# Layer 0's adjacency normalised with a graph in each partition, and group 0's sums read back in 128 rows

## The chip, the cores and the metric

The kernel runs on one core of a Trainium2 chip. The metric is the device time of one execution in microseconds (us), as the median of several runs. Engines are named as in the profile: PE is TensorE, DVE is VectorE, ACT is ScalarE, POOL is GpSimd, SP is the engine whose queue issues most of the transfers.

## The reference, cut to what matters

Four graph layers follow one another over 128 graphs of 64 nodes with 256 features, each with a residual and a layer norm. The change lies in layer 0. It works on the first 25 nodes of each graph, in five groups of nodes that overlap; each group has its own two-step graph convolution, and the groups' outputs are added with weights:

```
GROUPS = [list(range(25)), [0..8], [0, 9..14], [6, 7, 8, 12, 13, 14], [3, 4, 5, 9, 10, 11]]
def graph_conv(x, adj, W, b):
    A = adj + eye(n);  deg = sum(A, -1)
    dinv = where(deg == 0, 0, deg ** -0.5)
    return relu((dinv[:, :, None] * A * dinv[:, None, :]) @ (x @ W) + b)
for g, idx in enumerate(GROUPS):
    h = graph_conv(x[:, idx], adj[:, idx][:, :, idx], W1[g], b1[g])
    fused[:, idx] += softmax(fusion_w)[g] * graph_conv(h, adj_g, W2[g], b2[g])
x = layernorm(x + fused)          # nodes 25 to 63: only the norm of x
```

Layers 1 and 2 (a normalised convolution and a polynomial in the adjacency) and layer 3 (five steps of a gated recurrent cell over the graph) follow. Everything is float32.

## The kernel before, in words

**Units.** Layer 0 is cut into 16 units of up to four tiles. A tile holds as many graphs of one group as fit in the partitions, one row per node: 14 graphs of 9 nodes (group 1, units 0 to 2), 16 of 7 (group 2, units 3 and 4), 21 of 6 (groups 3 and 4, units 5 to 8), and 5 of 25 (group 0, units 9 to 15). For a unit i the steps are:

- `load0` brings the nodes' features xg (L447) and, for group 1, the rows of the adjacency a (L443).
- The block-diagonal, normalised and transposed adjacency AT is made in one of two ways. `prep` (L456) does it for units 0 to 2: identity, degree, power, the spread to blocks (L484), a transpose on TensorE (L492), and the second factor at the eviction (L497). For the others, `norm_group` (L517) normalises a whole group at once for all 128 graphs, in AL and AU, where each strip of 32 partitions holds nodes and 32 graphs lie along the row; VectorE's 32x32 block transpose (L533) turns it, SP stores it to DRAM as nt (L541), `load_turned` (L547) reads it back in the unit's row order, and `spread_out` (L561) multiplies it into blocks (L571).
- `aggregate` (L590) multiplies xg and AT; `hidden` (L606) or, from unit 3 on, `hidden7` (L629) multiplies by W1. `hidden7` takes seven products in place of eight, which need factors of W1 (`factors0`, L616, on POOL) and sums t of the aggregate (L634 to L636, on POOL), and copies c that ACT makes and DVE adds to (L665, the tile hg).
- `supports` (L685) multiplies by W2, `add` (L711) by AT again; its result z is added into F, the sums of groups 1 to 4, and for group 0 the sums F are added to z (L725).
- The sums of group 0 must come back from features-in-partitions to nodes-in-partitions. `finish` does it by TensorE's transpose (L778) for units 9, 14 and 15; for units 10 to 13, `turn_sum` (L739) turns z in 32x32 blocks on DVE (L744), stores it as zd (L748) and reads it back as zr (L750); `finish_turned` (L756) adds it (L759) and normalises.

`others` (L824) normalises nodes 25 to 63 in ten pieces, loaded by `load_others` (L799), stored as xb (L829).

**Order.** TensorE's instructions run in the order of the program throughout; from unit 2 on ACT, DVE and POOL do too, and that order is written out by hand in ORDER0 (L68), a row for each unit: P and F are `add` and its sum, A is `aggregate` of the next unit, digits are the products of `hidden7`, b, g, d and c its evictions, S is half of `supports`, L the loads for three units on, X `spread_out` for two units on, q a piece of the norms, e a piece of `mid`, the layers 1 and 2 of the first two chunks. SP's order, and all orders before unit 2, come from the scheduler, by its own costs and by priorities. [...]

**Shared places.** AL and AU have the tag RZ with two buffers; `ih` and `wl`, into which POOL loads the weights of layer 3 three at a time from unit 5 on (`moves`, L1040), take the same two buffers and wait until AL and AU are free. `a` has three buffers, xg five, W1 and W2 two each.

Of the kernel before, what the change touches and what calls it, by code (L numbers as in the profile page):

```python
# [28 lines left out]
NE = 15  # L29
# [36 lines left out]
WAITS = 6  # L66

ORDER0 = """  # L68
P A S q L 1 X 2 F 6 5 q 7 g S q 4 d 3 b c S S
A S 1 q q L q X q 2 5 q q 6 q S 7 P q S 4 q g q 3 q q S F b c d  # L70
q q A L P 1 S q S 6 2 q X 5 q q q 7 S S g F q b 4 q q 3 d c
A S P q L 1 X q S 6 F q q 2 5 q 7 q g S S 4 b q 3 q d c q q q
A P L 1 X S 6 2 q q 5 q S 7 F S q q 4 q g q q q d q q q b 3 c q S
X A q L P q S 1 q q q q q S q 6 F 2 q S q q 5 q q b q 7 q q S g 4 d 3 c
A q L q S X 1 S q 6 P 2 5 q 7 g S b 4 q q q d F q 3 q q S c q q
L X A P S 1 S 2 q 6 S 5 7 S q q q g 4 F 3 d q b c q
X P A L S 1 2 F q 6 5 q q q e 7 b g q q S q e 4 3 S q q q c S e q d e
X A L P 1 F 2 e q S 6 S q q b e e 5 q 7 S e g q q q 4 3 c S q e d e
L X P e A 1 F q S S 2 e e 6 5 q 7 q S q b q e 4 g q q q 3 e q S q d c q e e
L A e X P 1 2 F S 6 q q q q 5 S e 7 e S q g q 4 b q 3 q d q q S c q e q  # L80
X A S 1 e e L P 2 e e F 6 b 5 q q q q S 7 e g 4 S e q d q 3 q q q q e q c q e e S e
A L X e S 1 P 6 e q e q q q 2 5 F b e 7 S q q S 4 q e q e q g q q q 3 q e q S d c e
# [28 lines left out]
def gnn_stack(  # L111
# [305 lines left out]
    with ExitStack() as c0:  # L417
# [9 lines left out]
        def load0(i, after=None):  # L427
# [3 lines left out]
            qa = {0: [nc.sync, nc.scalar, nc.gpsimd, nc.sync], 1: [nc.sync, nc.scalar]}.get(i, [nc.sync])  # L431
            qx = nc.gpsimd if i < 3 else nc.sync
            a = work.tile([TR, 4, NJ], F32, name="a", bufs=3) if u.g == 1 else None
            xg = work.tile([TR, 4, D], F32, name="xg", bufs=5)
            w = u.n if u.g < 2 else NE
# [6 lines left out]
            for rows, t, b, f in runs if u.g == 1 else ():  # L442
                qa[t % len(qa)].dma_start(a[rows, t, :w], adj[b, f, 0:w])  # L443
# [12 lines left out]
        def prep(i):  # L456

            u = UNITS[i]
            a, xg = loads.pop(i)
            ae = work.tile([TR, 4, NJ], F32, name="ae", bufs=2)  # L460
            A0 = work.tile([TR, 4, TR], F32, name="A0", bufs=1)
            AT = work.tile([TR, 4, TR], F32, name="AT", bufs=4)
            p = psum0("pT").rearrange("p (t n) -> p t n", t=4)
            scale, last = [], evictions[-1] if evictions else None
            for ts, nb, r, k in u.same:
                w, c = ts.stop - ts.start, 0

                step = w if i else 2
                parts = [slice(t, min(t + step, ts.stop)) for t in range(ts.start, ts.stop, step)]
                for f, m in [(0, u.n)] if u.g < 2 else RUNS[u.g]:  # L470
                    with tc.issue_after(last.ins) if last else nullcontext():
                        nc.vector.tensor_add(
                            ae[:r, ts, c : c + m], a[:r, ts, f : f + m], eye0[:r, k, None, c : c + m].to_broadcast([r, w, m])
                        )
                    c += m
                av = ae[:r, ts, : u.n]
                deg = small.tile([TR, w], F32, name="deg")
                nc.vector.tensor_reduce(deg[:r], av, AX.X, ALU.add)
                dinv = inv_sqrt(deg[:r], w, r, "d0")
                nc.vector.tensor_mul(av, av, dinv[:, :, None].to_broadcast([r, w, u.n]))  # L480
                for ps in parts:
                    o, c, n = 0, 0, ps.stop - ps.start
                    for _, m in RUNS[u.g]:
                        nc.vector.tensor_mul(  # L484
                            A0[:r, ps, o : o + nb * m].rearrange("p t (b n) -> p t b n", n=m),
                            ae[:r, ps, None, c : c + m].to_broadcast([r, n, nb, m]),
                            block0[:r, None, k, o : o + nb * m].rearrange("p t (b n) -> p t b n", n=m)
                            .to_broadcast([r, n, nb, m]),
                        )
                        o, c = o + nb * m, c + m  # L490
                    for t in range(ps.start, ps.stop):
                        nc.tensor.transpose(p[:r, t, :r], A0[:r, t, :r], ident[:r, :r])  # L492
                    d = dinv[:, ps.start - ts.start : ps.stop - ts.start, None]
                    scale.append((AT[:r, ps, :r], p[:r, ps, :r], d.to_broadcast([r, n, r])))
            for v in scale:
                with tc.high_priority():
                    evictions.append(nc.vector.tensor_mul(*v))  # L497
            A[i] = AT, xg

        def identity(m):  # L500
            nc.vector.tensor_add(AL[:, :, :m], AL[:, :, :m], eye1[:, None, :m].to_broadcast([128, 32, m]))

        def degrees(g):

            deg = roots[:, 0, max(g - 1, 0)]
            if g == 2:
                nc.vector.tensor_reduce(deg, AL[:, :, 9:15], AX.X, ALU.add)
                nc.vector.tensor_add(deg, deg, AL[:, :, 0])
            elif g:
                seg = AU[:, 16:18, :].rearrange("p b n -> p (b n)").rearrange("p (b s) -> p b s", s=2)  # L510
                for s, (f, m) in enumerate(RUNS[g]):
                    nc.vector.tensor_reduce(seg[:, :, s], AL[:, :, f : f + m], AX.X, ALU.add)
                nc.vector.tensor_add(deg, seg[:, :, 0], seg[:, :, 1])
            else:
                nc.vector.tensor_reduce(deg, AL[:, :, 0:NJ], AX.X, ALU.add)

        def norm_group(g):  # L517

            n, o = len(GROUPS[g]), 0
            S = AS[len(nts) % 2]  # L520
            nts[g] = []
            degrees(g)
            deg, s, r = (roots[:, v, max(g - 1, 0)] for v in range(3))
            nc.vector.scalar_tensor_tensor(s, deg, 0.0, deg, op0=ALU.is_equal, op1=ALU.add)
            powers.append(nc.gpsimd.tensor_tensor(r, s, mhalf[:, :1].to_broadcast([128, 32]), ALU.pow))
            for _ in range(WAITS):
                yield
            nc.vector.scalar_tensor_tensor(s, deg, 0.0, r, op0=ALU.not_equal, op1=ALU.mult)
            d = s[:, :, None]
            for f, m in RUNS[g]:  # L530
                nc.vector.tensor_mul(S[:, :, f : f + m], AL[:, :, f : f + m], d.to_broadcast([128, 32, m]))
            yield
            nc.vector.transpose(AU.rearrange("p b n -> p (b n)"), S.rearrange("p b n -> p (b n)"))  # L533
            yield
            for f, m in RUNS[g]:
                nc.vector.tensor_mul(S[:, :, o : o + m], AU[:, :, f : f + m], d.to_broadcast([128, 32, m]))
                o += m
            for f, m in RUNS[g]:
                nt = dram.tile([B, m, n], F32, name=f"nt{g}{f}")
                for v in range(4):  # L540
                    nc.sync.dma_start(  # L541
                        nt[32 * v : 32 * v + 32].rearrange("b j i -> j b i"), S[32 * v + f : 32 * v + f + m, :, :n]
                    )
                nts[g].append(nt)
            yield

        def load_turned(i):  # L547
            u = UNITS[i]
            a = work.tile([TR, 4, NJ], F32, name="a", bufs=3)
            for ts, nb, _, _ in u.same:  # L550
                row, b0 = 0, u.tiles[ts.start][0]
                w = ts.stop - ts.start
                for nt, (_, m) in zip(nts[u.g], RUNS[u.g]):
                    nc.sync.dma_start(
# [184 lines left out]
        def turn_sum(i):  # L739
# [7 lines left out]
            for v in range(4):  # L747
                nc.sync.dma_start(zv[v], zt[32 * v : 32 * v + 32])  # L748
            zr = work.tile([TR, 4, D], F32, name="zr", bufs=1)
            nc.sync.dma_start(zr[: u0], zd[: 4 * u0].rearrange("(t r) d -> r t d", r=u0))  # L750
# [101 lines left out]
        def load_first(g):  # L852
            W1[g] = w0.tile([128, 2, HID], F32, name="W1", bufs=2)
            nc.sync.dma_start(W1[g], w1[g].rearrange("(k p) e -> p k e", p=128))
# [6 lines left out]
        nts, turned = {}, {}  # L861
        r1 = keep.tile([128, 2, 1024], F32, tag="RZ", name="AL", bufs=2).rearrange("p s (b n) -> p s b n", b=32)
        r2 = keep.tile([128, 2, 1024], F32, tag="RZ", name="AU", bufs=2).rearrange("p s (b n) -> p s b n", b=32)
        AL, AU, AS = r1[:, 0], r1[:, 1], [r2[:, 0], r2[:, 1]]
        eye1 = w0.tile([128, 32], F32, name="eye1")
        roots = w0.tile([128, 3, 4, 32], F32, name="roots")
        nc.vector.memset(AL, 0.0)

        def load_graphs(n, m):

            for v in range(4):
                nc.sync.dma_start(
                    AL[32 * v : 32 * v + n, :, :m], adj[32 * v : 32 * v + 32, :n, :m].rearrange("b i j -> i b j")
                )
# [13 lines left out]
        def stage(f, i, first=0):  # L888
            if first <= i < NU:
                f(i)  # L890
# [12 lines left out]
        for i in range(-2, NU + 1):  # L903
            if i == 2:
                written.enter_context(tc.manual_schedule(engines=free))
            if i == 1:
                factors0(2)
            if i == 0:
                first = norm_group(2)
# [712 lines left out]
```

## Time and profile before

| | us |
|---|---|
| median of three runs (2147.01 to 2149.83) | 2149.17 |
| the profiled execution's own time | 2147.78 |
| its span | 2146.0 |
| PE busy | 2099.1 |
| DVE busy | 1705.3 |
| ACT busy | 1001.0 |
| POOL busy | 653.6 |
| PE busy in the first 345 us, which hold layer 0 and the hand-over to layer 3 | 316.5 |

The mean granted TensorE clock was 0.991. The span is what the records cover; the profiled execution's own time has 1.8 us more around it. In a timeline, a line gives the start, the length, the engine (or its queue: SPq, POOLq, ACTq), the line of the program, the operation, output and inputs with their number, and in brackets the idle time before it and what ended it. In an answer by windows, a line gives the stretch, its length, the busy time of PE, PE's weight loads, DVE, ACT and POOL, then the granted TensorE clock, the share of the 16 DMA engines that were busy, and GB/s.

### The profile page before, as it was taken

The page shows a single profiled execution, that of the slowest core. Times are in us where ns is not written, and L with a number is a line of the kernel's source. Part 1 is how long each engine was busy: PE and PEld are TensorE (multiplying, and loading weights), DVE is VectorE, ACT ScalarE, POOL GpSimd, SP SyncE. Part 2 cuts the span into 40 slices and gives each one's busy share as a digit, 9 for nine tenths or more (in the row PEclk, how much of TensorE's full clock was granted, in tenths as well). Part 3 has the DMA queues.
Part 4 walks back from the last instruction along what each step waited for, and adds up shares of the span by engine and source line. Part 5 has one row for each costly group of instructions (what it writes and reads, how often), then busy time and mean ns, then how long its engine had stood idle before and what let it go on. Part 6 is the DMA issues. An engine that isn't in the chain of part 4 may idle for free.

```text
span 2146.0 us, 31812 instructions
## 1 busy us (share of the span) xinstructions
PE 2099.1 (98%) x10814; PEld 1843.2 (86%) x10814; DVE 1705.3 (79%) x3825; ACT 1001.0 (47%) x2097; POOL 653.6 (30%) x693
## 2 busy tenths in 40 slices
PE   9989889999999999999999999999999999999997
PEld 6879778898888888888888888888889888888886
DVE  4755666787897889788988898879888887888776
ACT  3545334444544445444544454445444454445453
POOL 7543212222232223232322322323322232223222
PEclk9999999999999999999999999999999999999999
DMA  6553220212522243223331332134312431224121
GB/s 174 151 143 83 68 71 21 70 40 55 108 65 51 60 79 86 50 52 74 87 74 40 74 86 68 45 73 86 79 45 55 90 84 40 59 59 97 44 59 40
DMA packets 551488, 154.73 MB, mean 72 GB/s; under 512 B 516160, under 2 KB 546350, under 8 KB 551326
## 3 DMA queue, kind: packets, MB, share of 16 engines
q1 hardware_dynamic: 546294, 147.46, 29.0%
q0 software_dynamic: 2320, 4.82, 0.9%
q8 instruction: 86, 1.41, 0.3%
q10 hardware_dynamic: 2712, 0.42, 0.1%
q14 instruction: 76, 0.62, 0.1%
HBM read 85.12 MB, written 67.49 MB: 71 GB/s over the span
## 4 chain that ended last, share of the span: by engine, by line
PE 79%; DVE 12%; DMA 4%; SPq 2%; issue 1%; POOL 1%; ACT 0%; DVEq 0%; POOLq 0%; ACTq 0%
PE parz L1168 22%; PE pdrz L1168 11%; PE pan L1168 11%; PE pa L272 8%; PE pdn L1168 5%; PE pbrz L1168 5%; PE pd L351 5%; PE ps L685 3%; PE pbn L1168 3%; PE ph L651 2%; DMA zr<-zd 1%; DVE NI L1326 1%; PE pp L332 1%; PE pf L881 1%; DVE NI L1327 1%
## 5 line engine op out<-in xcount | busy, mean ns | idle before, releaser
L1148 POOL TENSOR_TENSOR Ta<-agg 128x512 f32<-128x512 f32 x80 | 104.3, 1303 | 663.8 <-ACT agg L274 663.8
L1269 ACT ACTIVATE RZ<-RZ,brz 128x256 f32<-128x256 f32 x474 | 214.7, 501 | 169.0 <-DVE RZ L1192 168.3
L1168 PE MATMUL parz<-Th,WHH 128*128 128x256 f32 x960 | 288.6, 382 | 3.7 <-ACT c L1188 3.7
L1168 PE MATMUL parz<-Ta,V 128*128 128x256 f32 x960 | 285.5, 379 | 0.0
L1188 ACT COPY c<-parz 128x512 f32<-128x512 f32 x240 | 138.9, 579 | 269.2 <-PE parz L1168 268.3
L1284 ACT ACTIVATE NI<-NI,bih 128x256 f32<-128x256 f32 x316 | 149.2, 504 | 159.6 <-DVE NI L1327 159.5
L1188 ACT COPY c<-pan 128x512 f32<-128x512 f32 x237 | 138.2, 583 | 182.0 <-PE pan L1168 182.0
L1168 PEld LDWEIGHTS parz<-Th,WHH 128*128 128x128 f32 x960 | 179.6, 190 | 35.8 <-ACT c L1188 12.7
L1168 PEld LDWEIGHTS parz<-Ta,V 128*128 128x128 f32 x960 | 182.4, 190 | 24.8
L1148 POOL TENSOR_TENSOR Th<-hn 128x512 f32<-128x512 f32 x64 | 81.5, 1273 | 314.6 <-DVE hn L1291 310.3
L1289 DVE TENSOR_TENSOR RZ<-hn,NI 128x256 f32<-128x256 f32 x252 | 134.0, 532 | 34.5 <-ACT NI L1284 34.1
L1290 DVE TENSOR_TENSOR RZ<-RZ 128x256 f32<-128x256 f32 x316 | 150.9, 478 | 10.7
L1192 DVE TENSOR_TENSOR NI<-pdn,c 128x512 f32<-128x512 f32 x158 | 108.2, 685 | 56.7 <-ACT c L1188 54.6
L188 POOL TENSOR_TENSOR rs<-ve,mhalf 128x4 f32<-128x4 f32 (+2 forms) x65 | 69.5, 1070 | 256.4 <-DVE ve L181 187.1
L1327 DVE TENSOR_TENSOR NI<-NI 128x256 f32<-128x256 f32 x237 | 138.6, 585 | 8.2
L1168 PE MATMUL pan<-Ta,V 128*128 128x256 f32 x474 | 144.1, 385 | 0.1
L1168 PE MATMUL pan<-Th,WHH 128*128 128x256 f32 x474 | 141.0, 379 | 0.0
L1192 DVE TENSOR_TENSOR RZ<-pdrz,c 128x512 f32<-128x512 f32 x160 | 109.6, 685 | 37.1 <-PE pdrz L1168 25.3
L1326 DVE SCALAR_TENSOR_TENSOR NI<-NI,bhh,RZ 128x256 f32<-128x256 f32 x237 | 128.3, 541 | 6.3 <-ACT RZ L1269 1.4
L274 ACT COPY agg<-pa 128x512 f32<-128x512 f32 x160 | 93.3, 585 | 76.9 <-PE pa L272 76.3
L272 PEld LDWEIGHTS pa<-A,h 128*128 128x128 f32 x1024 | 124.5, 192 | 5.0 <-DMA h<-hb 1.6
L272 PE MATMUL pa<-A,h 128*128 128x128 f32 x1024 | 124.9, 275 | 1.5 <-DMA h<-hb 1.5
(267 smaller groups left out, 4874.8 us busy)
## 6 DMA issues: line engine op xcount, KB each, us to landing
hb<-flip SPq DMA_DIRECT2D x184, 256.0 KB
h<-hb SPq DMA_DIRECT2D x624, 64.0 KB
out_dram<-xt SPq DMA_DIRECT2D x30, 256.0 KB
hT<-hb SPq DMA_DIRECT2D x112, 64.0 KB
W<-in_w_dram SPq DMA_DIRECT2D x10, 512.0 KB
xt<-xb SPq DMA_DIRECT2D x32, 156.0 KB
xo<-in_x_dram SPq DMA_DIRECT2D x9, 512.0 KB
xb<-xo SPq DMA_DIRECT2D x9, 512.0 KB
```

The costliest lines, as they stand in the source:

```text
L272: nc.tensor.matmul(p[:, q * 128 : (q + 1) * 128], src(q, k), m[:, q, :], start=True, stop=True)
L351: nc.tensor.matmul(p[:, h, :], ag[:, k, q * 128 : (q + 1) * 128], W[:, k, :], start=k == 0, stop=k == 1)
L1148: nc.gpsimd.tensor_sub(t[:, 0:2, :], a[:, :, H:], a[:, 0, :].rearrange("p (s n) -> p s n", s=2))
L1168: nc.tensor.matmul(bank[:, g, :], w[:, q, i - 1, :], rhs, start=i in (1, 2, 5) and g == 0 and m == 0, stop=m == len(side) - 1, skip_group_ ...
L1188: nc.scalar.copy(c, self.a)
L1192: nc.vector.tensor_add(v, self.b if i == 2 else self.d, self.copies.pop({7: 7, 2: 1, 3: 6}[i]))
L1269: nc.scalar.activation(v, self.g.a[:, q, :] if i == 4 else v, AF.Sigmoid, bias=brz[:, 2 * q + j : 2 * q + j + 1])
L1284: nc.scalar.activation(n, n, AF.Tanh, bias=bih[:, 4 + j : 5 + j])
L1289: nc.vector.tensor_sub(d, self.hT[:, j, f], n)
L1290: nc.vector.tensor_mul(d, d, z)
L1326: nc.vector.scalar_tensor_tensor(n[:, j, f], h, bhh[:, 4 + j : 5 + j], r[:, j, f], op0=ALU.add, op1=ALU.mult)
L1327: nc.vector.tensor_add(n[:, j, f], i, n[:, j, f])
```

## The change

Only unit 0 keeps its adjacency from `prep`. For all groups, `norm_group` now works with one graph in each partition: AL holds the 25 used rows of each graph as they lie in DRAM, loaded in two pieces (rows 0 to 8, rows 9 to 24). The identity is added along the diagonal by one step with a stride of 65. Groups 2 to 4 are first copied together (L503 of the changed kernel); a degree sum, the guarded power of n columns, one product into S, and one product into T, whose operand S is read with its two inner axes exchanged, so that no block transpose is needed. T is stored as nt with one DMA for each run of nodes. Groups 2, 3, 4 and 0 are done together at unit 0; group 0 was done from unit 4 on. Units 1 and 2 take the way of `load_turned` and `spread_out`.

`turn_sum` stores zd and reads zr with priority; zr is four reads of 128 rows (rows t*125 to t*125+127, the last three of each unused) where it was one of 125 rows by four. ORDER0 has new rows. The loads of the other pieces, of W1 (with priority from group 2 on) and W2 have new places, the weight moves no longer wait for a power in the scheduler's order, and `load_adj(0)` comes after a read-back.

```diff
-WAITS = 6
 ORDER0 = """
-P A S q L 1 X 2 F 6 5 q 7 g S q 4 d 3 b c S S
-A S 1 q q L q X q 2 5 q q 6 q S 7 P q S 4 q g q 3 q q S F b c d
...
-L A e X P 1 2 F S 6 q q q q 5 S e 7 e S q g q 4 b q 3 q d q q S c q e q
...
+X q A P 1 q S L 2 6 5 b 7 S q g S F 3 4 c S d q
+X A S 1 2 q q 5 6 S L q q P 7 q S g q 4 F 3 q c S b q d
...
+X A e e P 1 2 L F 6 S q q q q e q 5 S 7 q S g b q 3 q 4 q d c q S q e q
...
@@ load0
-            qa = {0: [nc.sync, nc.scalar, nc.gpsimd, nc.sync], 1: [nc.sync, nc.scalar]}.get(i, [nc.sync])
+            qa = [nc.sync, nc.scalar, nc.gpsimd, nc.sync]
-            a = work.tile([TR, 4, NJ], F32, name="a", bufs=3) if u.g == 1 else None
+            a = None if i else work.tile([TR, 4, NJ], F32, name="a", bufs=3)
...
+        def load_graphs(lo, hi):
+            nc.sync.dma_start(AL[:, lo:hi, :], adj[:, lo:hi, :])
+
+        def identity(lo, hi):
+            d = graphs[:, : NJ * (N + 1)].rearrange("p (i k) -> p i k", k=N + 1)[:, lo:hi, 0]
+            nc.vector.tensor_scalar(d, d, 1.0, None, op0=ALU.add)
 
         def norm_group(g):
-            n, o = len(GROUPS[g]), 0
-            S = AS[len(nts) % 2]
...
+            n, o = len(GROUPS[g]), sum(len(GROUPS[v]) ** 2 for v in range(g))
+            S, T = (r2[:, v, o : o + n * n].rearrange("p (i j) -> p i j", j=n) for v in range(2))
+            C = AL[:, :n, :n]
+            if g > 1:
+                C, at = S, []
+                for f, m in RUNS[g]:
+                    at.append((sum(k for _, k, _ in at), m, f))
+                for i, k, f in at:
+                    for j, m, e in at:
+                        nc.vector.tensor_copy(S[:, i : i + k, j : j + m], AL[:, f : f + k, e : e + m])
+            deg, s, r = (roots[:, v, g, :n] for v in range(3))
+            nc.vector.tensor_reduce(deg, C, AX.X, ALU.add)
             nc.vector.scalar_tensor_tensor(s, deg, 0.0, deg, op0=ALU.is_equal, op1=ALU.add)
-            powers.append(nc.gpsimd.tensor_tensor(r, s, mhalf[:, :1].to_broadcast([128, 32]), ALU.pow))
-            for _ in range(WAITS):
-                yield
+            powers.append(nc.gpsimd.tensor_tensor(r, s, mhalf[:, :1].to_broadcast([128, n]), ALU.pow))
+            yield
             nc.vector.scalar_tensor_tensor(s, deg, 0.0, r, op0=ALU.not_equal, op1=ALU.mult)
-            d = s[:, :, None]
-            for f, m in RUNS[g]:
-                nc.vector.tensor_mul(S[:, :, f : f + m], AL[:, :, f : f + m], d.to_broadcast([128, 32, m]))
-            yield
-            nc.vector.transpose(AU.rearrange("p b n -> p (b n)"), S.rearrange("p b n -> p (b n)"))
...
+            nc.vector.tensor_mul(S, C, s[:, :, None].to_broadcast([128, n, n]))
+            turned_last = nc.vector.tensor_mul(T, S.rearrange("p i j -> p j i"), s[:, :, None].to_broadcast([128, n, n]))
             for f, m in RUNS[g]:
                 nt = dram.tile([B, m, n], F32, name=f"nt{g}{f}")
-                for v in range(4):
-                    nc.sync.dma_start(
-                        nt[32 * v : 32 * v + 32].rearrange("b j i -> j b i"), S[32 * v + f : 32 * v + f + m, :, :n]
-                    )
+                nc.sync.dma_start(nt, T[:, o : o + m, :])
...
@@ turn_sum
-            for v in range(4):
-                nc.sync.dma_start(zv[v], zt[32 * v : 32 * v + 32])
-            zr = work.tile([TR, 4, D], F32, name="zr", bufs=1)
-            nc.sync.dma_start(zr[: u0], zd[: 4 * u0].rearrange("(t r) d -> r t d", r=u0))
+            zr = work.tile([128, 4, D], F32, name="zr", bufs=1)
+            with tc.high_priority():
+                for v in range(4):
+                    nc.sync.dma_start(zv[v], zt[32 * v : 32 * v + 32])
+                for t in range(4):
+                    nc.sync.dma_start(zr[:, t, :], zd[t * u0 : t * u0 + 128])
@@ load_first
-            nc.sync.dma_start(W1[g], w1[g].rearrange("(k p) e -> p k e", p=128))
+            with tc.high_priority() if g > 1 else nullcontext():
+                nc.sync.dma_start(W1[g], w1[g].rearrange("(k p) e -> p k e", p=128))
...
             if i == 0:
-                first = norm_group(2)
+                rest = [norm_group(g) for g in (2, 3, 4, 0)]
                 with tc.issue_after(evictions[-1].ins):
-                    identity(15)
-                    next(first)
-            if i == 4:
-                load_graphs(NJ, NJ)
-            if i == 5:
-                identity(NJ)
+                    identity(9, NJ)
+                    for g in rest:
+                        next(g)
...
-            if i == 5:
-                todo.insert(0, (4, norm_group(0)))
...
                 with tc.issue_after(evictions[1].ins):
-                    prep(1)
+                    identity(0, 9)
+                    for _ in norm_group(1):
+                        pass
+                    load_turned(1)
+                    load_turned(2)
+                    spread_out(1)
...
+                with tc.issue_after(reads[2].ins):
+                    load_graphs(9, NJ)
+                    load_first(2)
+                    load_second(2)
+                    load_others(0)
...
             if i > 4:
-                with tc.issue_after(powers[-1].ins):
-                    for m in moves[3 * (i - 5) : 3 * (i - 4)]:
-                        nc.gpsimd.dma_start(*m)
+                for m in moves[3 * (i - 5) : 3 * (i - 4)]:
+                    nc.gpsimd.dma_start(*m)
...
             elif i == g0 - 1:
-                load_adj(0)
+                with tc.issue_after(reads[g0 - 2].ins):
+                    load_adj(0)
```

## The prediction

> **What bounds the kernel now.** I read the page first, for its engine shares and the chain.
>
> ```profile
> PE 2099.1 (98%) x10814; PEld 1843.2 (86%) x10814; DVE 1705.3 (79%) x3825; ACT 1001.0 (47%) x2097; POOL 653.6 (30%) x693
> PE 79%; DVE 12%; DMA 4%; SPq 2%; issue 1%; POOL 1%; ACT 0%; DVEq 0%; POOLq 0%; ACTq 0%
> ```
>
> TensorE bounds the whole: 2146.0 - 2099.1 = 47 us is all its idle time. The diff touches layer 0 and its hand-over alone, so I asked who TensorE waits for between 100 and 350 us (columns: waiting, released by, us in total, times, longest).
>
> ```profile
> PE ph L651 <- DVE hg L665: 8.5, 2, 7.3
> PE ph L651 <- POOL t L635: 8.0, 1, 8.0
> PE pse L778 <- DVE z L725: 4.0, 1, 4.0
> PE pa L272 <- DVE V L1136: 3.2, 1, 3.2
> ```
>
> Then the timeline of each engine around the two long stalls. First stall:
>
> ```profile
> 109.76 14.56 SPq L541 DMA_DIRECT2D nt<-AU  x4
> 130.06 2.27 POOL L1040 DMA_DIRECT2D wl<-in_wlT_dram  x3 [10.34 <-DMA a<-nt]
> 136.53 1.25 PE L651 MATMUL ph<-t,w 128*128 128x132 f32 x4 [8.00 <-POOL t L635]
> ```
>
> Group 0's adjacency leaves AU by four stores that need 14.56 us to issue. POOL, in order, stands 10.34 us at a weight load into AU's place; behind it are factors0 and the sums t that the products read. Second stall:
>
> ```profile
> 248.08 0.26 SPq L750 DMA_DIRECT2D zr<-zd  x1
> 254.63 1.29 DVE L759 TENSOR_TENSOR xg<-zr,xg 125x512 f32<-125x512 f32 x2 [8.26 <-DMA zr<-zd]
> 261.50 2.04 PE L651 MATMUL ph<-ag,w 128*128 128x250 f32 x4 [7.29 <-DVE hg L665]
> ```
>
> The read-back of the turned sums lands 6.55 us after its issue; VectorE waits in order, and the hg that TensorE needs is behind it. Two windows (length, busy times, granted clock, DMA share, GB/s):
>
> ```profile
> 136.50:142.00 5.50, 5.47 (x20) 4.85 (x21) 3.03 (x13) 1.08 (x3) 3.70 (x5) 0.56 0.51 139
> 251.00:252.00 1.00, 1.00 (x7) 0.88 (x6) 0.00 (x0) 0.74 (x2) 0.00 (x0) 1.00 0.34 122
> ```
>
> After an 8 us stall TensorE runs at about half clock; the zr read occupies a third of the DMA engines.
>
> [...]
>
> **Part by part.**
>
> *Removed: units 1 and 2 turned by TensorE.* In the chain their transposes stand at 0.43 and 0.22 us: gain 0.65. Nothing covers them; TensorE is busy on both sides.
>
> *Removed: the late group 0.* The strips of 32 graphs, two memsets, eight loads of AL and 28 stores of short runs go. In their place stand two loads of AL over 128 rows and one store for each run of a group (eight), all in the first 40 us. AU is then free long before the weight loads, which come near 107 us, so POOL waits there for nothing. Stall 1 goes: 8.0 idle, and the slow clock after it, which is 1.25 and 1.09 against 0.61 twice (L651 x4) and 3.33 against 1.89 (L685 x8) = 2.6. Gain 10.6. Next late there would be t behind factors0, which needs W1 of group 0; before issued that load at 109.0 and SP gets to it no later, while t is wanted at 126.
>
> *Moved: the ramp.* Units 1 and 2 now get their adjacency through DRAM. Unit 0's last AT ends at 9.66; identity, sum and guard 0.6; POOL is issuing xg until 10.79, then the power: 5.42 us for 32 columns and 1.03 for 4 give 0.157 a column, so 1.8 for 9: 12.7. Three VectorE steps 0.7; store and read back, each 2 to 5.44 us (the latter is the longest a<-nt landing in the chain): 18 to 24; spreading 0.7. TensorE wants AT at 25.3 (25.86 less 0.43). Zero, with 0 to 6 us to spare; each us beyond costs one. The start itself: W1 and AL (512 and 288 KB) are issued about 1.5 us earlier beside xg, which lands up to 6.2 us after its issue, about when TensorE reads it: 0 to 1, taken 0.5.
>
> *The wait that the change adds.* SP is in order. Behind the read-backs of units 1 and 2 (about 17.5) stand W1, AL and W2 of 0.5 MB each; [...]1 MB at 300 GB/s (the windows from 16 to 24 us moved 276 to 365) land AL near 23. After 2 us of VectorE's copies and sums, four powers (7, 6, 6 and 25 columns at 0.157 and a fixed 0.4: 8.5 us) bring POOL to 33.5; [...]. Then POOL has factors0, three memsets and four DMA issues (2.9 + 1.5 + 2.8) and only then the rs of the first other rows, about 41.7; VectorE applies it to 43.2; SP's store of those rows waits for that, and behind it stand unit 4's a and xg, unit 5's a and xg (eight and six issues, 4.7 to 7.2 us each set) and W1 of group 3: issued at 55 to 58, where before had it at 53.24. It lands 4 to 6.4 later (81.32 to 87.80 in before, where POOL waited for it): 59 to 64. POOL's factors0 (2.9) and unit 4's t (1.3) follow: 63.5 to 68.5. TensorE wants t at 64.6. Loss 0 to 4, taken 2. Unit 3's AT ends near 44 and is wanted at 46.4, unit 4's xg lands near 54 and is wanted at 59.4: zero.
>
> *zr in 128 rows.* In before the data runs about 4.3 us of the 6.55 to 6.97. [...] four issues at 0.5 to 0.6 replace one of 0.26. The first half lands 3.5 after the first issue, the second 4.8: gain 2.0 to 3.3 in each of four turns. With the priority, zd's stores go out together: at the second turn SP stood between the first (236.46) and the other three (242.62), behind xg loads. Turn 2: zt ends 235.8, stores 2.6 plus landing 3, reads to 246.5; VectorE is ready at 246.4, so 8.26 falls to about 0.3; hg then comes at about 253.1 and the new order asks for it at about 253.2 (one product sooner). Stall 2 was 7.29 plus clock (2.04 - 1.01) + (3.62 - 1.89) + (1.45 - 0.98) = 3.2, together 10.5; I leave 0.8: gain 9.7 (bounds 6 and 10.5). Turn 3: the 1.24 us gap goes: 1.2. Turn 4: zr was issued at 292.81 and used at 299.60; 2.7 earlier takes the 3.97 gap to 1.3. The 0.77 at L711 stays, and of the slow clock (1.99 for 0.98, L881 7.52 for 5.67: 2.9) 0.5 is left: gain 5.0 (bounds 2.5 and 7). The 3.2 at L1136 stays: it is the fold's own chain.
>
> *Reordering.* ORDER0 is rewritten in all fourteen rows with the same products; the sums t and the copies still have 2 to 4 us of other products between. Bounds -3 and +1 (TensorE is unbroken there now, so little can be gained); taken as a loss of 1. The other edits (the other rows' loads, load_adj and the moves' order) I cost at zero: TensorE's unbroken work hides their issues, and without that cover each costs its 0.3 to 0.8 us of issue.
>
> *Sum.* 0.65 + 10.6 + 9.7 + 1.2 + 5.0 - 0.5 - 2.0 - 1.0 = 23.7. The profiled execution took 2147.78 (span 2146.0 and 1.8 around it): 2124.1. The median of the three runs, 2149.17, is 1.4 above it: 2125.5, given as 2125.
>
> **Rivals.**
> *The first 70 us run late (chance 0.20).* For: four powers in a row on POOL, then SP's store waiting for the last of it, and every issue behind. If AL lands 4 us later than I think, W1 of group 3 does too, and the stall of about 6 brings the slow clock: 4 to 12 more, 2129 to 2137.
> *Stall 1 moves (0.07).* POOL's factors0 for group 0 stands before unit 8's t as before. If W1 of group 0 lands after about 120 instead of 113, TensorE stops in the same place for 5 to 8 us: 2131 to 2134. Against: SP has little else there.
> *The read-back is no faster (0.06).* The edit then does not do what it says: zr takes 6.8 us over 128 rows too. Turn 2 still gains about 5 from the order of stores, turn 4 about 0.5: 10 lost, 2135. Against: the share of 0.34.
> *Slower (0.03).* One mechanism: SP's in-order stand behind nt of unit 1 and the other rows' store. Every us that W1 of group 3 is issued after 57 costs one. The gain of the rest is 25.7 and the slow clock costs about 3, so it decides from an issue at about 80 on; I would see 2154. Against: SP's longest wait in the first 60 us of before is 2.4 us.
>
> **How the numbers follow.** Likeliest case 0.62: 2119 to 2130, its middle 2125. Losses that eat the whole gain and no more: 0.02. Low 2118 is stall 4 gone and no new wait; high 2136 takes in the late ramp and the slow read-back but their tail; about 0.15 lies outside. About 0.2% (4.3 us) is what a measurement can tell from no change: faster 0.95, within 0.02, slower 0.03.
>
> **What would show it.** Right: no wait of POOL at the wl load; no TensorE gap near 117 to 126; zr's DMA share near 1 for some 1.5 us, landing under 5; the clock 1.00 from 15 us to about 275. Wrong: TensorE waiting for t near 65 or for AT near 25 or 46, over 3 us; zr still 6.5; a VectorE wait on zr over 2 us at the second turn.

## The result, and the profile after

The changed kernel takes 2126.8 us (median of four runs, 2126.3 to 2127.2), beside 2149.5 for the kernel before (2147.0 to 2150.5): ratio 0.990, 95% interval 0.988 to 0.991. The prediction was 2125.0 with a range of 2118 to 2136. Its profiled execution took 2127.2 us with a span of 2125.5, so 20.5 us of the old span of 2146.0 are gone.

The page after, the same two lines as before:

```profile
PE 2092.4 (98%) x10808; PEld 1837.7 (86%) x10808; DVE 1686.4 (79%) x3808; ACT 1005.2 (47%) x2097; POOL 637.9 (30%) x686
PE 82%; DVE 11%; DMA 2%; POOL 2%; issue 1%; SPq 1%; ACT 1%; DVEq 0%; POOLq 0%; ACTq 0%
```

TensorE's idle time falls from 47 us to 33, its busy time by 6.7, which is mostly slow clock after the stalls that went (some 2.6 us at stall 1 and 3.2 at stall 2 by the prediction's lines) less what the new stall added. The transfers' share of the chain falls from 4% to 2%. Whom TensorE waits for between 100 and 350 us (waiting, released by, us in total, times, longest):

```profile
PE pa L271 <- DMA xg<-in_x_dram: 3.6, 1, 3.6
PE pa L271 <- DVE V L1105: 3.6, 1, 3.6
PE pse L754 <- DVE z L699: 2.2, 2, 1.8
PE pa L271 <- DVE xt L202: 0.9, 1, 0.9
```

Stalls 1 and 2 are gone. V L1105 is the hand-over's old wait (3.2 before); V holds the weights of layer 3's input, which the fold, products of `ih` and `wl`, makes at the hand-over. The first line is new, and no step of the prediction had it. POOL, where stall 1 was, issues the wl loads without a wait and stands idle before factors0 only until its buffer is free:

```profile
112.11 2.26 POOL L1008 DMA_DIRECT2D wl<-in_wlT_dram  x3
121.07 0.72 POOL L594 TENSOR_TENSOR w<-W 128x256 f32<-128x256 f32 x1 [6.69 <-PE ph L625]
```

At stall 2 the four stores of zd go out together, and VectorE finds zr there. At turn 4 it still waits:

```profile
231.41 2.76 SPq L724 DMA_DIRECT2D zd<-zt  x4
237.00 1.76 SPq L726 DMA_DIRECT2D zr<-zd  x4
```
```profile
240.23 1.81 DVE L735 TENSOR_TENSOR xg<-zr,xg 125x512 f32<-125x512 f32 x2
...
279.63 1.29 DVE L735 TENSOR_TENSOR xg<-zr,xg 125x512 f32<-125x512 f32 x2 [3.21 <-DMA zr<-zd]
```

The new stall is the first gather of layer 1. Its xt comes from the sums that SP stored as xa. SP's queue, then TensorE, of the changed kernel:

```profile
186.01 2.13 SPq L771 DMA_DIRECT2D xa<-xg  x4
192.94 1.32 SPq L256 DMA_DIRECT2D xt<-xa  x3
```
```profile
194.03 1.00 PE L331 MATMUL pp<-poly,An 128*128 128x64 f32 x8
198.67 3.42 PE L271 MATMUL pa<-AT,xt 128*128 128x128 f32 x16 [3.64 <-DMA xg<-in_x_dram]
201.88 1.28 PE L331 MATMUL pp<-poly,An 128*128 128x64 f32 x8
```

SP can load xt only when the stores have landed, 4.8 us after the last was issued. TensorE is at the gather at 195.03 and gets xt at 198.67 (the transfer that the profile names shares the queue with the load of xt; in a_zr125, a_noprio and a_pool5, which have the same steps here, it is xt<-xa by name). Sixteen matmuls then take 3.42 us where the kernel before has 2.00, at a granted clock of 0.51. Before, the same stores stood in two pairs, and the gather did not wait:

```profile
195.07 0.82 SPq L795 DMA_DIRECT2D xa<-xg  x2
196.67 0.91 SPq L795 DMA_DIRECT2D xa<-xg  x2
199.58 2.03 SPq L257 DMA_DIRECT2D xt<-xa  x3
```
```profile
204.56 2.00 PE L272 MATMUL pa<-AT,xt 128*128 128x128 f32 x16
```

There the first store goes out 0.9 us behind the start of unit 12's aggregate and xt's load 5.4 behind it; in the changed kernel, whose aggregate starts at 184.47, 1.5 and 8.5. TensorE is at the gather 10.4 us behind that aggregate before and 10.6 after. So the gather has not moved; the load of its data goes out 3.1 later.

To see where the time went I cut each trace at the same TensorE work: the aggregates of units 7, 9, 12 and 14, the first gather of the second set of graphs, and the first product of layer 3's gates (the tile parz). Rows of the written order move these marks by up to a microsecond against each other, so kernels with one order compare best. Length of each stage in us, from the timelines:

| kernel | to unit 7 | to 9 | to 12 | to 14 | to 2nd gather | to parz | rest |
|---|---|---|---|---|---|---|---|
| before | 105.5 | 39.6 | 49.0 | 46.1 | 36.2 | 70.3 | 1799.3 |
| after | 105.6 | 29.1 | 49.8 | 50.5 | 26.0 | 66.9 | 1797.6 |
| b_moves | 108.4 | 29.4 | 49.0 | 46.6 | 34.8 | 71.7 | 1798.2 |
| b_zr | 109.2 | 38.5 | 49.0 | 45.3 | 27.5 | 64.1 | 1796.8 |
| b_both | 105.5 | 30.9 | 49.0 | 45.5 | 27.4 | 65.7 | 1797.0 |
| a_xt | 105.3 | 29.1 | 49.8 | 47.3 | 26.0 | 66.9 | 1796.1 |
| a_zr125 | 105.7 | 29.1 | 49.8 | 49.8 | 32.6 | 70.5 | 1795.2 |
| a_noprio | 105.7 | 29.1 | 49.8 | 51.0 | 33.0 | 65.2 | 1797.2 |
| a_oldorder | 106.1 | 28.9 | 49.0 | 48.1 | 26.4 | 66.9 | 1795.8 |

After against before: 10.5 gained at stall 1, 0.8 and 4.4 lost in the two stages with the new row order and the new stall, 10.2 gained at turn 2, 3.4 at turns 3 and 4 and the hand-over (turn 3's gap, at 281.80 before, lies behind the second gather, which starts at 276.41), 1.7 in layer 3, which the diff does not touch.

### The profile page after: what moved, and what is told of

Its sections match the earlier page's. It is cut to its first block, busy times and chain, and to the rows that moved or that the text cites. A ratio compares the mean times of both kernels' runs of the same rounds, so it can differ in the third digit from the quotient of the medians.

```text
span 2125.5 us, 31755 instructions
## 1 busy us (share of the span) xinstructions
PE 2092.4 (98%) x10808; PEld 1837.7 (86%) x10808; DVE 1686.4 (79%) x3808; ACT 1005.2 (47%) x2097; POOL 637.9 (30%) x686
## 3 DMA queue, kind: packets, MB, share of 16 engines
q1 hardware_dynamic: 537275, 147.94, 28.9%
## 4 chain that ended last, share of the span: by engine, by line
PE 82%; DVE 11%; DMA 2%; POOL 2%; issue 1%; SPq 1%; ACT 1%; DVEq 0%; POOLq 0%; ACTq 0%
PE parz L1137 23%; PE pdrz L1137 12%; PE pan L1137 11%; PE pa L271 8%; PE pdn L1137 6%; PE pbrz L1137 5%; PE pd L350 5%; PE pbn L1137 3%; PE ps L659 3%; PE ph L625 3%; DVE NI L1295 1%; PE pp L331 1%; DVE NI L1296 1%; PE po L685 1%; PE pf L850 1%
```

## The experiments

The kernel before, run beside each group of experiments, had medians from 2146.9 to 2150.1; medians of different groups that lie under some 3 us apart are not told apart by the time alone.

Theory: two independent waits made the gain, POOL's stand behind group 0's late stores and the read-back of zd, and a third wait, the gather's, took some 5 us of it back. Rivals: the new way of turning the adjacency, or the new written order, is what gained; of the read-back, only the width of the transfer, or only its place on SP.

### b_moves: stall 1 cured without the new adjacency

```diff
-            if i > 4:
+            if i > 6:
...
-                    for m in moves[3 * (i - 5) : 3 * (i - 4)]:
+                    for m in moves[3 * (i - 7) : 3 * (i - 6)]:
```

> The kernel before, with the weight loads that go into AU's place issued two units later, so that POOL meets them when group 0's stores have long left; adjacency, read-back of the sums and the written order stay as before. Theory (stall 1 is POOL in order at the weight load behind those stores): no wait of POOL at the wl load, no TensorE gap before unit 8's products, 10.6 us less than before, about 2139. Rival (the stores themselves, VectorE's strips or SP's full queue hold unit 8 back, and POOL's stand is only beside it): the gap near 117 to 126 stays or moves to another wait, within 2 us of before, 2147 to 2150.

Measured: 2142.6 us (2138.6 to 2146.9), ratio 0.997 (0.996 to 0.998): 6.9 less. In the stage of stall 1 the gain is 10.2 of the 10.6 expected, and POOL has no wait at a weight load; its first two sets in b_moves:

```profile
132.63 2.18 POOL L1040 DMA_DIRECT2D ih<-in_wihT_dram  x3
144.47 2.26 POOL L1040 DMA_DIRECT2D wl<-in_wlT_dram  x3
```

Of what is missing, the profiled execution has 2.9 us in the ramp, which this edit does not touch: unit 3's aggregate waited for its adjacency. TensorE in b_moves and in b_both, which have the same code up to there, then VectorE's spread of unit 3 in b_moves and in before:

```profile
51.06 2.01 PE L590 MATMUL pa<-AT,xg 112*128 112x112 f32 x16 [2.04 <-issue]
```
```profile
48.73 1.94 PE L590 MATMUL pa<-AT,xg 112*128 112x112 f32 x16
```
```profile
50.26 0.69 DVE L571 TENSOR_TENSOR AT<-a,block 112x64 f32<-112x64 f32 x2 [3.76 <-DMA nt<-AU]
```
```profile
47.18 0.69 DVE L571 TENSOR_TENSOR AT<-a,block 112x64 f32<-112x64 f32 x2 [1.08 <-DMA a<-nt]
```

b_zr has it too (1.78), before does not. So the old ramp has a wait that comes in some executions and costs 3 to 4 us (2.9 in b_moves, 3.7 in b_zr). Ten profiles with the new adjacency reach unit 7 at 105.2 to 106.1, four with the old one at 105.5 to 109.2.

### b_zr: the read-back alone

The kernel before with the changed kernel's turn_sum, and nothing else.

> The kernel before, with only the read-back of group 0's sums changed: four reads over 128 rows, and its stores and reads put first on SP; stall 1 stays. Theory: stall 2 goes (10.0), turn 3 gives 0.8, turn 4 gives 3.9, together 14.7 less: about 2135, zr landing in 3.5 to 4.5 us instead of 6.5 to 7, VectorE waiting for zr under 4 us in all instead of 19. Rival (the late turns gain because everything ahead of them runs sooner or because the written order is new): under 7 us gained, 2143 or more.

Measured: 2131.3 (2129.8 to 2132.2), ratio 0.992 (0.990 to 0.993): 18.1 less, 3.4 more than expected. The stages of turns 2 to 4 give 8.7 and 6.2, 14.9 together, as expected; its profiled execution gained 2.5 more in layer 3 and lost 3.7 in the ramp. VectorE's waits for zr fall from 19.4 to 7.8 in all, not to under 4; of stall 2, 7.29 before, TensorE keeps 1.59:

```profile
257.56 1.11 PE L651 MATMUL ph<-ag,w 128*128 128x250 f32 x4 [1.59 <-DVE hg L665]
```

The rival falls: neither the new adjacency nor the new order is needed for this part.

### b_both: the two together

> The two kernels above in one: weight loads two units later and the new read-back, the adjacency of layer 0 and the written order as before. Theory: the two gains add, 10.6 + 14.7 = 25.3, about 2124, so the new way of turning the adjacency is worth no more than a later place for the loads; it may end 1 to 4 below the changed kernel, which has a new wait at the first gather of layer 1. Rival (turning by the order of reading gives time of its own on the path, in the ramp or in VectorE's load): this kernel ends 4 or more above the changed one, 2131 or more.

Measured: 2124.4 (2122.8 to 2125.4), ratio 0.989 (0.987 to 0.990): 25.1 less, the sum of 6.9 and 18.1. A few lines of edits in the old kernel give what the whole change gives, within the noise. The rival would have had 2131 or more.

### a_xt: the gather later

```diff
-X A L P 1 F 2 e S S 6 e b e e e 5 7 S g q q 3 ...
+X A L P 1 F 2 e S S 6 e b 5 7 S e e e g q q 3 ...
```

> The changed kernel, with the first gather of layer 1 and the two steps behind it moved behind product 5, product 7 and two tiles' support in the row of unit 11 (3.8 us of TensorE's work that now stands after them). Theory (the gather waits 3.64 us for xt, which SP can load only when the first unit's sums have landed in DRAM, and the clock drops for some 1.5 us after it): the gap goes, 4 to 5.5 less than the changed kernel, about 2122. Rival (the step moved back makes layer 1's chain of the first graphs late, or the wait stands there anyway): the gap shows up at L350 or later with the same size, within 1 us of the changed kernel, 2126 to 2128.

Measured: 2123.2 (2122.4 to 2123.9), ratio 0.988 (0.986 to 0.989): 3.6 less than the changed kernel, a little under the 4 expected. TensorE now has 3.8 us of other work there, the gather does not wait and runs at full clock:

```profile
196.31 1.89 PE L659 MATMUL ps<-W,hg 128*125 128x256 f32 x8
198.03 1.95 PE L271 MATMUL pa<-AT,xt 128*128 128x128 f32 x16
199.81 1.05 PE L331 MATMUL pp<-poly,An 128*128 128x64 f32 x8
202.89 1.11 PE L625 MATMUL ph<-ag,w 128*128 128x250 f32 x4 [2.03 <-DVE hg L639]
```

Part of it came back: a wait of 2.03 for hg, since the work that covered hg's eviction was spent before the gather.

### a_zr125 and a_noprio: width and place apart

```diff
-                for t in range(4):
-                    nc.sync.dma_start(zr[:, t, :], zd[t * u0 : t * u0 + 128])
+                nc.sync.dma_start(zr[:u0], zd[: 4 * u0].rearrange("(t r) d -> r t d", r=u0))
```

> The changed kernel, with the sums read back in one transfer over 125 rows as before, its place on SP kept. Theory (the width of the read is what brings the sums earlier): zr lands 6.5 to 7 after its issue instead of 4.3; at turn 2 VectorE waits some 3 us, at turn 4 the wait of 3.2 becomes 5.5 and TensorE's gaps after it grow by as much, with a slow clock: 4 to 8 more than the changed kernel, 2131 to 2135. Rival (the place of the stores and the read on SP is what counts): within 1.5 of the changed kernel, 2125.5 to 2128.5.

a_noprio instead drops `with tc.high_priority():` around the stores and the four reads.

> The changed kernel, with the four reads over 128 rows kept but the stores and reads no longer put first on SP: by the order of SP's instructions only turn 2 differs, where three of the four stores stand behind two loads of xg. Theory of the width alone: within 1.5 of the changed kernel. Theory of both: the reads of turn 2 go out 3 to 5 us later (about 241 instead of 237), VectorE waits 3 to 6 us there and TensorE 2 to 5: 3 to 7 more, 2130 to 2134.

Measured: a_zr125 2134.2 (2133.6 to 2134.9), ratio 0.993 (0.991 to 0.994), 7.4 above the changed kernel; a_noprio 2132.6 (2128.9 to 2134.5), ratio 0.992 (0.990 to 0.993), 5.8 above. Both are needed: with either edit taken away about half of the stall of turn 2 comes back (3.88 and 3.82 us of the old 7.29). SP, VectorE and TensorE at turn 2 in a_zr125:

```profile
237.76 0.27 SPq L725 DMA_DIRECT2D zr<-zd  x1
```
```profile
244.50 1.29 DVE L734 TENSOR_TENSOR xg<-zr,xg 125x512 f32<-125x512 f32 x2 [4.79 <-DMA zr<-zd]
```
```profile
251.52 2.03 PE L625 MATMUL ph<-ag,w 128*128 128x250 f32 x4 [3.88 <-DVE hg L639]
```

and in a_noprio, where two loads of xg stand between the stores:

```profile
232.01 0.58 SPq L723 DMA_DIRECT2D zd<-zt  x1
235.45 1.64 SPq L445 DMA_DIRECT2D xg<-in_x_dram  x2
237.14 2.92 SPq L723 DMA_DIRECT2D zd<-zt  x3
242.57 1.77 SPq L725 DMA_DIRECT2D zr<-zd  x4
```
```profile
252.67 2.03 PE L625 MATMUL ph<-ag,w 128*128 128x250 f32 x4 [3.82 <-DVE hg L639]
```

In the first the data comes 6.7 us after its issue; in the second within 2.6 of the first issue, but that issue comes 5.0 later than in the changed kernel, counted from unit 14's aggregate. In both TensorE's 3.8 us of idle is followed by four matmuls in 2.03 instead of 1.01. The two stages of turns 2 to 4 are 10.2 longer in a_zr125, 5.3 in a_noprio: turn 4 needs the width alone.

### a_oldorder: the rows of the written order

The changed kernel with the fourteen rows of before.

> The changed kernel with all fourteen rows of the written order as in the kernel before. The prediction took the new rows as a loss of 1 us. If they are neutral but for the first gather of layer 1, which the old row has one support later, the gap of 3.64 there falls under 2 without a slow clock: 2 to 4.5 less than the changed kernel, 2122 to 2125. Rival (the new rows fit the new loads and are a gain of their own): above the changed kernel, 2129 or more, with waits for AT, t or the copies that it doesn't have.

Measured: 2122.2 (2120.4 to 2123.7), ratio 0.987 (0.986 to 0.988): 4.6 less than the changed kernel: the new rows are a loss, not a gain of their own. The traces put 2.4 of it in the gather's stage and 0.8 in the stage before; 1.8 lie in layer 3, where the rows do not reach. The expectation was wrong on why: the old row does not have the gather later (10.8 us behind the aggregate against 10.6). It has the stores earlier and in two pairs, since VectorE scales two tiles at a time, and xt's load goes out 7.3 behind the aggregate instead of 8.5:

```profile
184.91 1.15 SPq L771 DMA_DIRECT2D xa<-xg  x2
186.85 0.81 SPq L771 DMA_DIRECT2D xa<-xg  x2
191.30 1.55 SPq L256 DMA_DIRECT2D xt<-xa  x3
```
```profile
196.26 2.02 PE L271 MATMUL pa<-AT,xt 128*128 128x128 f32 x16 [1.43 <-DMA zd<-zt]
```

The gather still waits 1.43, without a slow clock behind it, and its stage is 2.0 longer than in the kernel before; that part is not the rows'. The other traces agree: with the new rows and the gather in its new place it waits 2.2 to 3.6 in all five, with the old rows and the new adjacency 1.4 or less in all four. Against b_both, which has the same rows, no gain of the new adjacency is shown: the medians (2122.2 and 2124.4) are too close, the profiled spans are 2121.2 and 2121.1, and what a_oldorder gains in the stage of stall 1 (2.0, where b_both has a wait of 1.77 for a ScalarE copy) it loses at the gather (2.6).

### a_pool and a_pool5: VectorE beside POOL

In the changed kernel VectorE's two products for group 0, of 625 elements, took 1.38 and 1.71 us, with factors0 on POOL beside them; in the kernel before those of 800 elements took 0.99 (L531) and 0.98 (L536). Here factors0 comes first:

```diff
-                with tc.issue_after(powers[-1].ins):
+                with tc.issue_after(evictions[-1].ins):
                     factors0(2)
```

> The changed kernel, with POOL's factors0 for group 2 ahead of the four powers instead of behind them, so that VectorE's products for group 0 (625 elements each) lie beside POOL's memsets and DMA issues and not beside its tensor_tensors. If POOL's tensor_tensors are what stretches the products (1.38 and 1.71 us in the changed kernel[...]), they take 0.8 to 1.0 here. If it is their strided reads, 1.4 to 1.7 stay. The time is not the question; the powers end some 3 us later, so up to 3 us may be lost at the first other rows' store and what stands behind it.

Changed kernel, then a_pool:

```profile
31.86 0.70 DVE L511 TENSOR_TENSOR AU<-AU,roots 128x36 f32<-128x36 f32 x1
32.49 1.38 DVE L510 TENSOR_TENSOR AU<-AL,roots 128x625 f32<-128x625 f32 x1
33.90 1.71 DVE L511 TENSOR_TENSOR AU<-AU,roots 128x625 f32<-128x625 f32 x1
```
```profile
33.12 0.21 DVE L511 TENSOR_TENSOR AU<-AU,roots 128x36 f32<-128x36 f32 x1
33.24 0.81 DVE L510 TENSOR_TENSOR AU<-AL,roots 128x625 f32<-128x625 f32 x1
34.08 1.36 DVE L511 TENSOR_TENSOR AU<-AU,roots 128x625 f32<-128x625 f32 x1
```

With POOL's memsets beside them the first product falls from 1.38 to 0.81 and the small one from 0.70 to 0.21; the second still takes 1.36. It reads S with rows and columns exchanged, and POOL issues two loads beside it (from 34.27). That the exchanged read is why it is slower is not shown, but the small groups point to it: 0.24 and 0.30 us for the two products of 81 elements in the changed kernel and 0.18 and 0.21 for those of 36 in a_pool, so the second takes 0.7 to 0.9 ns more for each element at all three sizes. The one execution took 2123.2 us; six more of the same kernel:

> The kernel of a_pool again, now timed: its one execution took 2123.2, 3.6 less than the changed kernel's median, of which its trace has 1.4 at the first gather of layer 1 (a wait of 2.2 instead of 3.64) and 2.5 at the hand-over. If that was the landing of two transfers, which differs from execution to execution, the median is 2125 to 2127.5. If the earlier factors0 is a gain of its own (POOL free some 3 us earlier from 33 on), it stays at 2122 to 2124.5.

Measured: 2124.7 (2123.7 to 2127.3), ratio 0.989 (0.988 to 0.991). The interval holds the changed kernel's 0.990, so no gain of time is shown. Its trace gives 0.80 and 1.34 for the two products once more.

### o_fold, o_all and o_whh: the hand-over's wait

The prediction left the hand-over's wait (3.2 before) alone as the fold's own chain. WHH holds the factors of the weights that the cell applies to its state hT. o_fold is a_oldorder with the evictions of the fold put first:

```diff
+                with tc.high_priority():
-                nc.vector.tensor_add(w[:, 4, :], p[:, 0, 128:256], w[:, 3, :])
-                nc.vector.tensor_sub(w[:, 6, :], w[:, 0, :], p[:, 0, 128:256])
+                    nc.vector.tensor_add(w[:, 4, :], p[:, 0, 128:256], w[:, 3, :])
+                    nc.vector.tensor_sub(w[:, 6, :], w[:, 0, :], p[:, 0, 128:256])
```

> The changed kernel with the old written order, and at the hand-over VectorE's two evictions of each product of the fold put ahead of the factors that are worked out from them. TensorE stands 3.57 us there (PE pa L271 behind V L1105), because the bank it needs is read only after 1.53 + 1.57 + 1.07 us of factors. Theory (the order of VectorE's steps is what ends that wait): the gap falls under 1.5 and the slow clock after it (32 products in 8.46 us[...]) goes, 2 to 4 less than a_oldorder, 2118 to 2120.5. Rival (the prediction's: the wait is the fold's own chain, and stays): within 1, 2121 to 2123.

Measured: 2122.5 (2119.4 to 2123.4), ratio 0.988 (0.986 to 0.990), no change against a_oldorder. The wait for V is gone, and TensorE stands as long one product later, while VectorE stands at the load of WHH with an eviction behind it (o_whh, below, tries that):

```profile
304.88 8.83 PE L850 MATMUL pf<-ih,wl 128*128 128x256 f32 x32 [3.22 <-issue]
```
```profile
302.10 0.64 DVE L1111 TENSOR_TENSOR WHH<-WHH,wh 128x384 f32<-128x384 f32 x1 [2.51 <-DMA WHH<-in_whhT_dram]
303.24 1.03 DVE L1110 TENSOR_TENSOR WHH<-wh,WHH 128x384 f32<-128x384 f32 x1 [0.50 <-DMA WHH<-in_whhT_dram]
```

> o_fold with ScalarE's copies of the same products put first too, and POOL's factors0 for group 2 ahead of the powers as in a_pool. If both are worth something: 1 to 3 below o_fold, 2116 to 2119. If neither: within 1 of o_fold.

Measured: 2127.3 (2124.1 to 2129.5), ratio 0.990 (0.989 to 0.992), 4.8 above o_fold: with the copies first, ScalarE's copy of hT comes late (a wait of 1.92 for hT L1182) and the other wait grows to 4.03. Both theories miss.

```diff
-                if q == 2 and l == 0:
+                if q == 2 and l == 1:
+                    with tc.issue_after(e.ins):
```

o_whh puts the four steps on WHH behind the second layer's last eviction, e.

> o_fold, with the four steps that make WHH's factors put behind the second layer's evictions. In o_fold the wait for V went, but TensorE stood 3.22 us one product later: VectorE, in order, waited 2.51 and 0.50 us for the load of WHH, with an eviction of V behind it. Theory (that load is what was left of the wait): no TensorE gap over 1 us between 297 and 315, the 32 products in 7.5 us instead of 8.8, 3 to 4.5 less than o_fold. Rival (the next eviction waits for something else still): the gap moves again, within 1 us of o_fold.

Measured: 2118.7 (2117.4 to 2119.3), ratio 0.986 (0.984 to 0.988): 3.9 less than o_fold, and the fastest kernel here, 8.1 below the changed one. No gap is left at the 32 products:

```profile
301.76 7.14 PE L850 MATMUL pf<-ih,wl 128*128 128x256 f32 x32
```

## Why the prediction was right, and where its sum was off

Step by step, as the prediction put it, in the profiled executions.

- *Start and transposes, +0.65 - 0.5; W1 of group 3 late, -2.0.* Unit 7 begins at 105.59 instead of 105.54: together -0.05. hidden(0) starts 0.34 later. W1 was issued at 56.69 as worked out (55 to 58) and t made TensorE wait 0.39: the loss was 0.4 of a taken 2.0, inside its 0 to 4 (by its own terms t would have been ready at 63.2 to 68.2, not 63.5 to 68.5; nothing hangs on that). What the prediction did not see is that the old ramp has a wait of its own in some executions, 3 to 4 us (b_moves, b_zr); the new one showed none.
- *Stall 1, +10.6.* Measured 10.5, and the cause is shown by b_moves: the place of the loads alone gives 10.2 in that stage. The rival that it moves to W1 of group 0 did not come about.
- *Turn 2, +9.7.* Measured 10.2. The prediction named both the width and the order of the stores; what the width would bring was the author's estimate, and in the rival the order alone got about 5. In the stage of turn 2 the order alone gives 3.6 (a_zr125) and the width alone 3.2 (a_noprio): most of the gain comes only with both.
- *Turn 3, +1.2; turn 4, +5.0.* With the hand-over, 3.4 of 6.2. Turn 4's own gap shrank more than forecast (3.97 to 0.46, where 1.3 was worked out) and turn 3's from 1.24 to 0.46; zr lands 4.3 after its first issue, inside the author's estimate of 3.5 to 4.8. What the prediction did not have are the waits behind them: VectorE still waits 3.2 for zr at turn 4, TensorE now waits 0.93 for xt and 1.78 for z, and the hand-over's wait is 3.56 where 3.17 stood. That wait stayed, as forecast, but not for the reason given: it is no chain of the fold's own, since o_whh, with VectorE's steps in another order, has no gap there.
- *Reordering, -1.0.* This term was mis-sized: the two stages lost 5.2, of which a_oldorder gives back 3.2. The prediction asked of the new rows whether t and the copies still have products between them and their use, and bounded the cost at -3. It did not ask when the transfers are issued that feed the early steps "e". VectorE now scales all four tiles before the first store, which goes out 0.6 us later behind the aggregate, and from the first store to xt's load it is 6.9 us instead of 4.5; 3.6 us of idle followed, and slow clock on top (a_xt takes both away). So the sign that the clock would be 1.00 up to about 275 did not hold. How long the stores take is settled in part only: four in a row took 5.4 to 6.9 in the six kernels with the new rows, two pairs 5.5 to 6.4 in the four with the old rows and the new adjacency, and 4.5 to 5.0 in the four with the old adjacency. So the pairing is not shown to matter, and what makes the stores of the new adjacency land later stays open; it is the 2 us that the old rows do not give back.
- *Layer 3, 0.* 1.7 was gained there. The diff does not touch it, and eight profiles of kernels that all leave its code alone have 1795.2 to 1798.2, so the execution of before was a long one (it has a wait of 1.5 for h<-hb, the others 0.5 or less). The cause stays open beyond that.

That the total came so close is in part luck, because errors met: the order cost 4.2 more than taken, turns 2 to 4 gave 2.3 less, the start 1.8 more and layer 3 an unexplained 1.7: 3.2 too much in all of 23.7. The mechanisms of the two large gains were right, and none of the rivals came about. No gain of the largest edit, the new adjacency, by turning faster is shown: it empties AU early, which later loads do as well, and its ten profiles show a steadier ramp.

## What to carry to other kernels

When an engine that works in order stands at a load into reused memory, ask first whether the load is merely early: moving it can do what a rewrite does (10.2 us in b_moves, 10.5 with the rewrite). A read-back through DRAM has three places, the store's issue, the read's issue and the read's width, and they have to be looked at together: at turn 2 the place alone gave 3.6 us, the width alone 3.2, both 10.2. After an order is rewritten, compare for each step that reads a transfer how far ahead of it the transfer's source is stored, and keep matmuls to put before the step whose data comes last.

## What the runs showed of the hardware

- VectorE's products of two operands took 1.38 us for 625 elements and 0.70 for 36 in the changed kernel, where POOL ran products beside them, and 0.81 and 0.21 in a_pool, where POOL ran memsets. At the hand-over L1083 took 1.53 in a_oldorder and 0.55 in o_fold; there POOL ran no product beside either and issued loads beside both, so the cause of that stretch stays open.
- What a gap of TensorE does to its clock is not settled by its length alone. Of the 19 gaps of 3.1 us and more in the fourteen traces' first 350 us, 18 were followed by slow matmuls (four in 2.03 for 1.01 after 3.88; clock 0.51 from 199 to 202 after 3.64), and one, of 3.56 in a_pool, was not (32 products in 7.07). In the kernel before the granted clock was 0.56 from 136.5 to 142 after the gap of 8.00, 0.50 from 261.5 to 267 after that of 7.29, and 1.00 from 281.8 to 284 after that of 1.24. Shorter gaps came both ways: 1.78 in the changed kernel left the clock at full (8 products in 1.89), 1.78 in b_zr did not (8 in 3.21), nor did 2.24 in a_pool (16 in 3.45 for 2.00), while 2.80 in a_oldorder did. In the changed kernel the wait of 3.64 cost 1.7 more in the matmuls behind it.
- The four reads of 128 rows kept the DMA engines 0.83 busy from 238 to 240 in the changed kernel (the prediction had near 1 for some 1.5 us), the one of 125 rows 0.34 from 240 to 244 in a_zr125, at 264 against 120 GB/s.
